# Reordering one step of an edge-gated graph layer: the add a tile ahead, expansion first, aggregation last

## The chip, the cores and the metric

The kernel runs on one core of a Trainium2 chip. The metric is the device time of one execution in microseconds (us); lower is better. Five engines work side by side: TensorE (PE in the profile, with its weight loads as PEld), VectorE (DVE), ScalarE (ACT), GpSimd (POOL, here the issuer of gathers) and SyncE (SP, an issuer of plain transfers). Each works through its own list of instructions in order and waits for others by semaphores.

## The reference

For each of 16 batches, 1024 nodes with 256 features `h`. Every pair of nodes (u, v) gets a gate, and the adjacency `A`, which is nearly empty (about nine entries per node, the diagonal among them), weighs it:

```python
pre_u = h @ W1[:256];  pre_v = h @ W1[256:]
hidden = relu(pre_u[:, :, None] + pre_v[:, None, :] + b1)
S = sigmoid(hidden @ W2 + b2)                 # one number for each u, v
a_t = einsum('buv,bud->bvd', S * A, h)        # gated sum over u
m_t = einsum('uv,bud->bvd', A, h) * h         # plain sum over u
out = beta1*h + beta2*(a_t @ Wa + ba) + beta3*(m_t @ Wm + bm)
```

## The kernel before

Only pairs with a non-zero adjacency are computed. The edges of a node tile of 128 v are put into lists, 10 tiles of up to 128 edges: two windows (`w`) of 64 v, five tiles (`j`) each. Batches go in four groups of four. One group with one node tile is a **block** (32 in all), one edge tile of a block is a **step** `n` (10 to a block, 320 in all); `s` is n mod 10. For a whole group the kernel first writes a table with a row of 2,048 numbers for each node u: `pre_u` of the four batches and, behind it, `h` of the four batches. Tables of later groups and lists of later node tiles are made in between the steps of earlier ones, up to about step 233.

Per step there are these pieces, all functions inside the kernel:

- `fetch(n)` (L496, POOL): an indirect DMA gathers the 128 table rows of the edges into one of six buffers `fetched`. It can start when the step that used the buffer six tiles ago is aggregated.
- `expand(n)` (L569, PE): two products with a 0/1 matrix `mark` spread `pre_v + b1`, which lies in `X`, over the edges, into one of two PSUM tiles `pc`.
- `gate(n)` (L601, L606 on DVE; L609, L612 on ACT): VectorE adds the gathered `pre_u` and `pc` into a tile `t`; four products, one per batch, take the ReLU times `W2` and sum along the row into `sc`. ScalarE takes the sigmoid `gt` and scales, once per batch, the weights in the tile `left`.
- `left_adj(n)` (L579, ACT): the unscaled half of `left`, the adjacency values at their places.
- `aggregate(n)` (L623, PE): products of `left` with the gathered `h`, 8 instructions where the tile touches one quarter of the window (j = 0 and 4), 16 where it touches two; they accumulate in PSUM in `acc0` and `acc1`.
- `half_end` (L631, ACT): after j = 2 and j = 4, thus after n with s = 2, 4, 7 and 9, a finished half is copied out of PSUM into `ev`.

Beside these a step holds work for whole blocks. What TensorE makes there is copied by ScalarE: transposes of `ev` into `LT` (L641, L644) at s = 1 (for the block before), 7 (two halves) and 9; the output products (L672, copies to `z` L675) at s = 3 to 6; the next block's `X` and its split `low` (L427, L461, L462 at s = 0 and 2, casts L465 at 3 and L468 at 5 and 6); table rows (L427, L443), in the middle of the run at s = 1 and 8; at s = 1 and 6 ScalarE also makes the next `mark` (L562). VectorE's part of it (L654, L676, L463) and the output transfers are put off by one to three steps through `after` and come up in `do(n)`.

The order of instructions on each engine is written by hand (`manual_schedule`): it is the order in which the main loop calls these functions. In step n the loop calls aggregate(n-1), two gathers of adjacency values (`fetch_val`, L382), fetch(n+5), half_end where due, gate(n), left_adj(n+1), load_mark, do(n), expand(n+2), and then the block's work.

Of the kernel before, what the change touches and what calls it, by code (L numbers as in the profile page):

```python
# [7 lines left out]
FP = mybir.dt.float32  # L8
# [3 lines left out]
ALU = mybir.AluOpType  # L12
AX = mybir.AxisListType
P = 128
# [3 lines left out]
def kernel(  # L18
# [42 lines left out]
    nc = tc.nc  # L61
    B, N, D = x.shape
    NT = N // P
    DC = D // P
    GB = 4
    NG = B // GB
    GD = GB * D
    W = 64
    NW = P // W
    TW = 5  # L70
# [58 lines left out]
    MID = TW // 2  # L129
# [81 lines left out]
    one = main.enter_context(tc.tile_pool(name="one", bufs=1))  # L211
# [17 lines left out]
    NF = 6  # L229
    EARLY = 4  # L230
    fetched = []
# [147 lines left out]
    def fetch_val(n):  # L379

        for i, j in wanted[:n]:
            nc.gpsimd.indirect_dma_start(  # L382
                out=val[:, i, j:j + 1], out_offset=None, in_=adj_flat,
                in_offset=bass.IndirectOffsetOnAxis(ap=vidx[:, i, j:j + 1], axis=0),
                bounds_check=N * N - 1, oob_is_err=False)
        del wanted[:n]
# [91 lines left out]
    def go(gen, step):  # L478

        try:  # L480
            gen.send(step)
        except StopIteration:
            pass
# [5 lines left out]
    def where(n):  # L489
        k, s = divmod(n, T)  # L490
        w, j = divmod(s, TW)
        return k, *order[k], w, j

    def fetch(n):
        k, g, vt, w, j = where(n)
        nc.gpsimd.indirect_dma_start(  # L496
            out=fetched[n % NF], out_offset=None, in_=table[g],
            in_offset=bass.IndirectOffsetOnAxis(ap=uidx[:, vt * NW + w, j:j + 1], axis=0),
            bounds_check=N - 1, oob_is_err=False)
# [55 lines left out]

    marks, pcs, accs, evs, hbs, LTs, lefts = {}, {}, {}, {}, {}, {}, {}

    def load_mark(q):  # L560
        marks[q] = big.tile([P, E], FR, name="mark")
        nc.scalar.copy(marks[q], whose[:, order[q // NW][1] * NW + q % NW, :])  # L562

    def expand(n):
        k, g, vt, w, j = where(n)
        pcs[n] = psc.tile([P, GD], FP, name="pc")
        for h in range(2):
            c = slice(2 * h * D, (2 * h + 2) * D)
            nc.tensor.matmul(pcs[n][:, c], marks[n // TW][:, j * P:(j + 1) * P], cuts[k][:, w, c],  # L569
                             start=True, stop=True)  # L570


    def left_adj(n):
        k, g, vt, w, j = where(n)
        i = vt * NW + w
        m = len(QUARTERS[j])
        o = max(2 * j - 1, 0)
        lefts[n] = wk.tile([P, 2, GB, 2, V], FP, name="left")
        nc.scalar.activation(lefts[n][:, :m, :, 0, :], onehot[:, i, o:o + m, :].unsqueeze(2).to_broadcast([P, m, GB, V]),  # L579
                             AF.Copy, scale=val[:, i, j:j + 1])  # L580
# [11 lines left out]
    def fill(n, gap=True):  # L592
        for r in running:
            if r[1] == gap and r[2] <= n:
                piece_of(r, n)
                break

    def gate(n):
        k, g, vt, w, j = where(n)
        t = one.tile([P, GB, D], FP, name="t")  # L600
        nc.vector.tensor_tensor(t, fetched[n % NF][:, :GD].rearrange("p (b d) -> p b d", b=GB),  # L601
                                pcs.pop(n).rearrange("p (b d) -> p b d", b=GB), ALU.add)
        sc = wk.tile([P, GB], FP, name="sc")
        for b in range(GB):
            fill(n)
            nc.vector.scalar_tensor_tensor(t[:, b, :], t[:, b, :], 0.0, w2_b,  # L606
                                           ALU.max, ALU.mult, accum_out=sc[:, b:b + 1])
        gt = wk.tile([P, GB], FP, name="gt")
        nc.scalar.activation(gt, sc, AF.Sigmoid, bias=b2_b)  # L609
        for b in range(GB):  # L610
            m = len(QUARTERS[j])
            nc.scalar.activation(lefts[n][:, :m, b, 1, :], lefts[n][:, :m, b, 0, :], AF.Copy, scale=gt[:, b:b + 1])  # L612

    def aggregate(n):
        k, g, vt, w, j = where(n)
        left, f = lefts.pop(n), fetched[n % NF]
        for i, q in enumerate(QUARTERS[j]):
            h, r = divmod(q, 2)
            first = j == h * MID and r == 0
            if first:  # L620
                accs[h] = psa.tile([P, 2, D], FP, name=f"acc{h}")
            for b in range(GB):
                nc.tensor.matmul(accs[h][b * 2 * V:(b + 1) * 2 * V, r, :],  # L623
                                 left[:, i, b].rearrange("p k v -> p (k v)"), f[:, GD + b * D:GD + (b + 1) * D],
                                 start=first, stop=(j == q + 1), skip_group_check=True)


    def half_end(n, q):

        evs[q] = one.tile([P, 2, D], FP, name=f"ev{q}")  # L630
        nc.scalar.copy(evs[q], accs.pop(q))  # L631
# [110 lines left out]
        expand(n)  # L742
    left_adj(0)
    total = BS * T
    for n in range(total + 2):
        k, s = divmod(n, T)
        if 1 <= n <= total:
            aggregate(n - 1)
            fetch_val(2)
            if n - 1 + NF < total:  # L750
                fetch(n - 1 + NF)
            if n % TW in (0, MID + 1):
                half_end(n - 1, 0 if n % TW else 1)
        if n < total:
            gate(n)
            if n + 1 < total:
                left_adj(n + 1)
        if n % TW == 1 and n // TW + 1 < total // TW:
            load_mark(n // TW + 1)
        do(n)  # L760
        if n + 2 < total:
            expand(n + 2)
        if n == 1:
            w_a = load_weights(Wa, "w_a", nc.sync)
            w_m = load_weights(Wm, "w_m", nc.sync)
            bias = load_rows(bm, D, "bias", nc.sync)
            ba_b = load_rows(ba, D, "ba_b", nc.sync)
            be1 = load_rows(beta1, 1, "be1", nc.sync)
            be2 = load_rows(beta2, 1, "be2", nc.sync)
            be3 = load_rows(beta3, 1, "be3", nc.sync)  # L770
            after(10, scale_late)
        if s == 0 and 0 < k < BS:
            hbs[k - 1] = big.tile([P, GB, D], FP, name="h_blk", bufs=1)
            g, vt = order[k - 1]
            nc.sync.dma_start(hbs[k - 1], x_rows[vt * P:(vt + 1) * P, g * GB:(g + 1) * GB, :])
        if n == total - 6:
            hbs[BS - 1] = hts.tile([P, GB, DC, P], FP, name="hT").rearrange("p b c n -> p b (c n)")
            for v, m, f in tails:
                for h, o in tail_rows(x, v, m, f):
                    nc.sync.dma_start(h, o)  # L780
        for i in advance.get(n, ()):
            next(made[i], None)
        if n in start_list:
            running.append([made[start_list[n]], True, n])
            piece_of(running[-1], n)
        fill(n, False)
        if (s == 1 and 0 < k < BS) or n == total:
            turn_over(k - 1, 1, 1, n)
        if s in (3, 4, 5, 6) and 0 < k < BS:
            if s == 3:  # L790
                end = block_end(k - 1)
                next(end)
            go(end, n)
        if s == 7 and k < BS:
            turn_over(k, 0, 0, n)
            turn_over(k, 0, 1, n)
        if s == 9 and k < BS:
            turn_over(k, 1, 0, n)
        if n == total - 2:
            end = tail(tails[:2], n)  # L800
            next(end)
        elif n == total - 1:
            go(end, n)
        elif n >= total:
            end = tail([tails[2 + n - total]], n)
            next(end)
            go(end, n)
            go(end, n)
        if k + 1 < BS and s in (0, 2, 3, 5, 6):
            if s == 0:  # L810
                parts = halves(k + 1)
                next(parts)
            go(parts, n)
        if n in loads:
            if loads[n] in begun and loads[n][0] == 1:
                aside_.remove(loads[n])
            load_hT(loads[n])
            if loads[n] not in begun:
                copy_h(loads[n])
                begun.add(loads[n])  # L820
        if n in at:
            if at[n] != last:
                last = at[n]
                piece = rows(last)
                next(piece)
            go(piece, n)
        if n == 120:
            nc.gpsimd.partition_all_reduce(longest, rest, P, bass_isa.ReduceOp.max)
            after(n + 12, count_rest)
# [7 lines left out]
    with tc.If(any_left > 0):  # L837
        with ExitStack() as s2:
# [3 lines left out]
            for vt in range(NT):  # L842
# [21 lines left out]
                with tc.For_i(0, n_turns, 1):  # L864
# [9 lines left out]
                    for g in range(NG):  # L874
# [4 lines left out]
                        sc = fw.tile([P, GB], FP, name="fb_sc")  # L879
# [64 lines left out]
```

## Time and profile before

| | |
|---|---|
| time, median of 3 runs | 1151.51 us (1146.13 to 1153.36) |
| profiled execution, span from first to last instruction | 1165.8 us (its own device time is not given apart) |
| PE busy | 1092.1 us, 94% |
| DVE busy | 1056.2 us, 91% |
| ACT busy | 893.5 us, 77% |
| POOL busy | 439.9 us, 38% |
| data moved | 391.40 MB, mean 336 GB/s |
| mean granted TensorE clock | 0.976 |

A line of a group names the line of the kernel, the engine and operation, what is written and read, and how often; then its busy time in us, the mean of one in ns, and the idle time just before such instructions with what ended it. A line of the waits has the waiting instruction, the one that released it, the time in total, how often and the longest. A line of the timeline has start and length in us, then the instructions, merged where the same follow each other (`x4`); a bracket gives the idle time ahead of them.

### The profile page before, as it was taken

The numbers are of one execution on the slowest core, as the hardware profiler recorded it, in microseconds if no ns is written. First come the engines' busy times: TensorE is split into PE (matmuls) and PEld (weight loads), VectorE is DVE, ScalarE is ACT, GpSimd is POOL, SyncE is SP. The second block draws the span as 40 slices with busy tenths as digits, with TensorE's granted clock in tenths as the row PEclk, the third lists the DMA queues.
The fourth block names the chain that finished last, engine by engine and source line by source line (L and its number), as shares of the span: only waits on it lengthen the run. The fifth ranks groups of instructions, "written<-read, shape, count | busy, mean of one in ns | idle before, by whom it ended". The sixth has DMA issues, their size and how long they took to land. (4 is left out here: it accounts for less than half of the span.)

```text
span 1165.8 us, 23918 instructions
## 1 busy us (share of the span) xinstructions
PE 1092.1 (94%) x7633; PEld 723.1 (62%) x7633; DVE 1056.2 (91%) x3487; ACT 893.5 (77%) x2624; POOL 439.9 (38%) x428
## 2 busy tenths in 40 slices
PE   7867899999999999999999999999999999999986
PEld 6744666666666666666666666666666666666553
DVE  7688889888999989999999999999999999999994
ACT  2346587767887878888888888888888888888873
POOL 1556645253335333443333333333333333333330
PEclk9868899999999999999999999999999999999999
DMA  9986898999999999999999999999998998999991
GB/s 286 298 307 223 277 372 312 362 320 331 342 320 323 396 379 336 358 350 402 389 374 369 355 364 356 360 364 383 371 375 324 361 322 333 334 339 328 328 346 60
DMA packets 147048, 391.40 MB, mean 336 GB/s; under 512 B 16753, under 2 KB 105329, under 8 KB 110705
## 3 DMA queue, kind: packets, MB, share of 16 engines
q0 software_dynamic: 50016, 300.50, 68.9%
q1 hardware_dynamic: 81616, 74.99, 20.0%
q10 hardware_dynamic: 15280, 14.29, 3.7%
q8 instruction: 63, 1.03, 0.3%
q14 instruction: 73, 0.59, 0.1%
HBM read 393.78 MB, written 50.33 MB: 381 GB/s over the span
## 5 line engine op out<-in xcount | busy, mean ns | idle before, releaser
L496 POOL DMA_INDIRECT fetched<-table,uidx x320 | 341.5, 1067 | 628.3 <-PE acc L623 447.2
L606 DVE SCALAR_TENSOR_TENSOR t<-t,w_b 128x256 f32<-128x256 f32 x1280 | 478.3, 421 | 19.3 <-ACT left L612 0.5
L601 DVE TENSOR_TENSOR t<-fetched,pc 128x1024 f32<-128x1024 f32 x320 | 389.3, 1217 | 41.4 <-PE pc L569 13.9
L623 PE MATMUL acc<-fetched,left 128*32 128x256 f32 x4096 | 336.2, 391 | 31.9 <-ACT left L612 26.2
L612 ACT ACTIVATE left<-left,gt 128x32 f32<-128x32 f32 (+1 forms) x1280 | 299.3, 304 | 10.4
L569 PE MATMUL pc<-X,mark 128*128 128x512 f32 x640 | 237.6, 453 | 6.2 <-ACT mark L562 5.0
L623 PEld LDWEIGHTS acc<-fetched,left 128*32 128x32 f32 x4096 | 130.6, 109 | 179.3 <-issue 52.4
L569 PEld LDWEIGHTS pc<-X,mark 128*128 128x128 f32 x640 | 97.2, 191 | 140.0 <-issue 89.3
L609 ACT ACTIVATE gt<-sc,b_b 128x4 f32<-128x4 f32 x320 | 96.2, 301 | 43.4 <-DVE t L606 40.8
L672 PE MATMUL misc<-w_m,LT 128*128 128x256 f32 x496 | 117.2, 379 | 0.0
L672 PE MATMUL misc<-w_a,LT 128*128 128x256 f32 x496 | 117.1, 379 | 0.0
L579 ACT ACTIVATE left<-onehot,val 128x128 f32<-128x128 bf16 (+1 forms) x320 | 116.5, 364 | 0.0
L427 PE MATMUL misc<-w_v,hT 128*128 128x256 f32 x448 | 107.3, 383 | 0.0
L427 PE MATMUL misc<-w_u,hT 128*128 128x256 f32 x416 | 101.2, 390 | 5.7 <-ACT few L329 3.6
L606 DVE DVE_READ_ACCUMULATOR t<-t,w_b 128x1 f32 x1280 | 104.0, 81 | 0.0
L672 PEld LDWEIGHTS misc<-w_a,LT 128*128 128x128 f32 x496 | 93.9, 189 | 15.1
L672 PEld LDWEIGHTS misc<-w_m,LT 128*128 128x128 f32 x496 | 93.8, 189 | 14.9
L382 POOL DMA_INDIRECT val<-in_adjT_dram,vidx x80 | 85.7, 1071 | 35.1 <-issue 22.4
L427 PEld LDWEIGHTS misc<-w_v,hT 128*128 128x128 f32 x448 | 86.0, 192 | 13.9
L427 PEld LDWEIGHTS misc<-w_u,hT 128*128 128x128 f32 x416 | 79.5, 195 | 17.3 <-ACT few L329 3.7
L631 ACT COPY ev<-acc 128x512 f32<-128x512 f32 x128 | 75.5, 590 | 14.6 <-PE acc L623 4.2
L675 ACT COPY z<-misc 128x512 f32<-128x512 f32 x62 | 36.3, 586 | 58.1 <-PE misc L672 38.8
(164 smaller groups left out, 947.9 us busy)
## 6 DMA issues: line engine op xcount, KB each, us to landing
h_blk<-in_x_dram SPq DMA_DIRECT2D x31, 512.0 KB
out_dram<-z SPq DMA_DIRECT2D x31, 512.0 KB
hT<-in_xT_dram SPq DMA_DIRECT2D x28, 512.0 KB
table<-in_x_dram ACTq DMA_DIRECT2D x24, 512.0 KB
table<-tab SPq DMA_DIRECT2D x24, 512.0 KB
fetched<-table,uidx POOLq DMA_INDIRECT x320
table<-in_x_dram SPq DMA_DIRECT2D x8, 512.0 KB
table<-fetched SPq DMA_DIRECT2D x8, 512.0 KB
```

The source lines that it names most:

```text
L382: nc.gpsimd.indirect_dma_start(out=val[:, i, j:j + 1], out_offset=None, in_=adj_flat, in_offset=bass.IndirectOffsetOnAxis(ap=vidx[:, i, j: ...
L427: nc.tensor.matmul(p[:, bb * D:(bb + 1) * D], hT[:, 2 * h + bb, i, :], wt[:, i, :], start=(i == 0 and not begun), stop=(i == DC - 1), skip ...
L496: nc.gpsimd.indirect_dma_start(out=fetched[n % NF], out_offset=None, in_=table[g], in_offset=bass.IndirectOffsetOnAxis(ap=uidx[:, vt * NW ...
L569: nc.tensor.matmul(pcs[n][:, c], marks[n // TW][:, j * P:(j + 1) * P], cuts[k][:, w, c], start=True, stop=True)
L579: nc.scalar.activation(lefts[n][:, :m, :, 0, :], onehot[:, i, o:o + m, :].unsqueeze(2).to_broadcast([P, m, GB, V]), AF.Copy, scale=val[:, ...
L601: nc.vector.tensor_tensor(t, fetched[n % NF][:, :GD].rearrange("p (b d) -> p b d", b=GB), pcs.pop(n).rearrange("p (b d) -> p b d", b=GB), ...
L606: nc.vector.scalar_tensor_tensor(t[:, b, :], t[:, b, :], 0.0, w2_b, ALU.max, ALU.mult, accum_out=sc[:, b:b + 1])
L609: nc.scalar.activation(gt, sc, AF.Sigmoid, bias=b2_b)
L612: nc.scalar.activation(lefts[n][:, :m, b, 1, :], lefts[n][:, :m, b, 0, :], AF.Copy, scale=gt[:, b:b + 1])
L623: nc.tensor.matmul(accs[h][b * 2 * V:(b + 1) * 2 * V, r, :], left[:, i, b].rearrange("p k v -> p (k v)"), f[:, GD + b * D:GD + (b + 1) * D ...
L631: nc.scalar.copy(evs[q], accs.pop(q))
L672: nc.tensor.matmul(pz[:, bb * D:(bb + 1) * D], LTs[k][:, c, 2 * h + bb, i, :], wt[:, c, :], start=False, stop=(i == 0 and c == DC - 1), sk ...
```

## The change

VectorE's add becomes a function of its own, `add(n)`, that writes in place of the gathered half of the buffer; the tile `t` is gone, and the four products work in the buffer too. `add(0)` runs ahead of the loop, and step n then calls add(n+1) before the products of n. The scalings move to a function `weigh(n)`. The aggregation with its fetches and `half_end` moves to `gather_in`. Step n now calls expand(n+2), add(n+1), gate(n), load_mark, do(n), the block's work, gather_in(n-1), weigh(n), left_adj(n+1).

```diff
+    def add(n):
+        t = fetched[n % NF][:, :GD]
+        nc.vector.tensor_tensor(t, t, pcs.pop(n), ALU.add)
+
     def gate(n):
         k, g, vt, w, j = where(n)
-        t = one.tile([P, GB, D], FP, name="t")
-        nc.vector.tensor_tensor(t, fetched[n % NF][:, :GD].rearrange("p (b d) -> p b d", b=GB),
-                                pcs.pop(n).rearrange("p (b d) -> p b d", b=GB), ALU.add)
+        t = fetched[n % NF][:, :GD].rearrange("p (b d) -> p b d", b=GB)
         sc = wk.tile([P, GB], FP, name="sc")
         for b in range(GB):
             fill(n)
             nc.vector.scalar_tensor_tensor(t[:, b, :], t[:, b, :], 0.0, w2_b,
                                            ALU.max, ALU.mult, accum_out=sc[:, b:b + 1])
+        scs[n] = sc
+
+    def weigh(n):
+        k, g, vt, w, j = where(n)
+        sc = scs.pop(n)
         gt = wk.tile([P, GB], FP, name="gt")
         nc.scalar.activation(gt, sc, AF.Sigmoid, bias=b2_b)
...
     total = BS * T
+    add(0)
+
+    def gather_in(n):
+        aggregate(n)
+        fetch_val(2)
+        if n + NF < total:
+            fetch(n + NF)
+        if (n + 1) % TW in (0, MID + 1):
+            half_end(n, 0 if (n + 1) % TW else 1)
+
     for n in range(total + 2):
         k, s = divmod(n, T)
-        if 1 <= n <= total:
-            aggregate(n - 1)
-            fetch_val(2)
-            if n - 1 + NF < total:
-                fetch(n - 1 + NF)
-            if n % TW in (0, MID + 1):
-                half_end(n - 1, 0 if n % TW else 1)
+        if n == total:
+            gather_in(n - 1)
+        if n + 2 < total:
+            expand(n + 2)
         if n < total:
+            if n + 1 < total:
+                add(n + 1)
             gate(n)
-            if n + 1 < total:
-                left_adj(n + 1)
         if n % TW == 1 and n // TW + 1 < total // TW:
             load_mark(n // TW + 1)
         do(n)
-        if n + 2 < total:
-            expand(n + 2)
...
+        if n < total:
+            if n:
+                gather_in(n - 1)
+            weigh(n)
+            if n + 1 < total:
+                left_adj(n + 1)
```

More of the change, by code (lines that the diff above doesn't have):

```diff
@@ L553, in scale_late @@
         nc.vector.tensor_scalar(w_m, w_m, be3, None, ALU.mult)
+    scs = {}
     marks, pcs, accs, evs, hbs, LTs, lefts = {}, {}, {}, {}, {}, {}, {}
```

## The prediction

> **What bounds the kernel now.** I read the page's engine shares first, then the groups, the waits of a middle stretch, and the timeline of TensorE (PE) and ScalarE (ACT).
>
> ```profile
> PE 1092.1 (94%) x7633; PEld 723.1 (62%) x7633; DVE 1056.2 (91%) x3487; ACT 893.5 (77%) x2624; POOL 439.9 (38%) x428
> ...
> L606 DVE SCALAR_TENSOR_TENSOR t<-t,w_b 128x256 f32<-128x256 f32 x1280 | 478.3, 421 | 19.3 <-ACT left L612 0.5
> L601 DVE TENSOR_TENSOR t<-fetched,pc 128x1024 f32<-128x1024 f32 x320 | 389.3, 1217 | 41.4 <-PE pc L569 13.9
> ```
>
> TensorE and VectorE (DVE) are both near full, so small bubbles decide. VectorE's waits from 310 to 870 us:
>
> ```profile
> DVE t L601 <- PE pc L569: 3.3, 9, 0.5
> DVE key L249 <- DMA key<-in_adjT_dram: 2.8, 1, 2.8
> DVE t L601 <- DMA fetched<-table,uidx: 2.1, 2, 1.7
> ```
>
> In 560 us it waits some 10 us for others. Now TensorE from step 6 to step 8 of a block (a block is ten steps; n is the tile, s = n mod 10):
>
> ```profile
> 601.72 1.89 PE L672 MATMUL misc<-w_m,LT 128*128 128x256 f32 x8
> 603.54 1.07 PE L623 MATMUL acc<-fetched,left 128*32 128x256 f32 x16
> 604.54 0.73 PE L569 MATMUL pc<-X,mark 128*128 128x512 f32 x2
> 605.11 1.03 PE L641 MATMUL misc<-ident,ev 128*128 128x128 f32 x8
> 606.08 1.65 PE L623 MATMUL acc<-fetched,left 128*32 128x256 f32 x16
> 607.65 0.73 PE L569 MATMUL pc<-X,mark 128*128 128x512 f32 x2
> 608.95 1.69 PE L623 MATMUL acc<-fetched,left 128*32 128x256 f32 x16 [0.56 <-ACT left L612]
> ```
>
> and ScalarE beside it:
>
> ```profile
> 602.75 0.71 ACT L562 CAST mark<-whose 128x640 fp32r<-128x640 uint8 x1
> 603.65 0.59 ACT L675 COPY z<-misc 128x512 f32<-128x512 f32 x1 [0.19 <-PE misc L672]
> 604.26 1.05 ACT L468 CAST X<-low 64x1024 fp32r<-64x1024 f32 x1
> 605.33 0.30 ACT L609 ACTIVATE gt<-sc,b_b 128x4 f32<-128x4 f32 x1
> 605.66 0.96 ACT L612 ACTIVATE left<-left,gt 128x32 f32<-128x32 f32 x4
> ...
> 606.82 1.04 ACT L644 COPY LT<-misc 128x512 f32<-128x512 f32 x2
> 607.76 0.59 ACT L631 COPY ev<-acc 128x512 f32<-128x512 f32 x1
> 608.24 0.30 ACT L609 ACTIVATE gt<-sc,b_b 128x4 f32<-128x4 f32 x1
> 608.57 0.96 ACT L612 ACTIVATE left<-left,gt 128x32 f32<-128x32 f32 x4
> ```
>
> An aggregation of 16 products takes 1.07 us when its scalings are there, 1.65 when it must follow them as they come: the stall sits inside "busy". It ends where a step's products are few and ScalarE's chain (copies, sigmoid, four scalings) is longer than what TensorE has left to do.
>
> Summing TensorE's start-to-start distances at their undisturbed values over all steps gives 31.1 us of work per block in n = 60 to 239 (18 blocks), which takes 32.7; from n = 240 (8 blocks), where no table rows are made, 27.7 of 31.2. The rest is stall. VectorE's floor per block, from the timeline's distances: add to first product 10 x 1.26, between products 30 x 0.35, last product to what follows 4.3, and the block's own work (z 2 x 0.66, low 1.14, LT 2 x 0.60) 3.7, together 31.0. So **VectorE sets the last 8 blocks, and the TensorE-ScalarE loop, closely followed by VectorE, the 18 in the middle**.
>
> **What the Trainium skill says.** "Perfetto Trace Analysis", Per-engine timelines: a matmul's end in a profile is estimated, not observed; agreed, the 1.65 above is spread starts. "TensorE: Matmul & The Clock Gate", Architectural detail: ScalarE and VectorE are strict first-in first-out; agreed: VectorE finished tile 147's products at 601.87, but its sigmoid starts at 605.33, behind mark, z and cast. "VectorE: DVE Perf Modes", The DRAIN you can't avoid: a semaphore after each VectorE operation costs nothing. This trace differs: an add followed by its own products, which wait for it, is 1.24 to 1.33 us from start to start, and 1.14 when an unrelated operation follows; a product followed by the next add is 0.52, by an unrelated operation 0.35. "DMA: Bandwidth & Descriptors", Specifications: 16 engines reach 435 GB/s; the page has 336 on average, 402 in its best slice.
>
> **The change, part by part.** VectorE's adds, products, scalings and matmuls keep their number and size.
>
> *The add one tile ahead, in place.* The stream becomes add(n+1), products(n). Neither waits for the instruction just before it, so about 0.12 per add and 0.17 on half of the last products go: 0.2 us a step, VectorE's floor falls from 31.0 to 29.0 per block. In the last 8 blocks this is worth up to 2 us each, if nothing else is late; in the middle nothing, as the loop of TensorE and ScalarE binds at once. Dropping tile t costs nothing: the add wrote 1,024 elements before too.
>
> *TensorE's order.* Before, cyclically: aggregate(n-1), expand(n+2), products(n). After: aggregate(n-1), expand(n+3), products(n+1). Only the pairing shifts: **each aggregation now follows the next step's products, and ScalarE's ev copy, sigmoid and scalings of n come behind the copies of step n, no longer of n-1**. I walked one block both ways with the timeline's distances (products 0.215 each, aggregation 0.26 or 0.69 from first to last start, expansion 0.335 + 0.23, hand-over to or from an aggregation 0.31; on ScalarE 0.48 per 128x512 copy, cast 1.07, mark 0.62, sigmoid 0.33, scalings 0.96, left 0.29; matmul to copy 0.42; the last start of a delayed 16-product aggregation 0.73 after the last scaling). The walk of before gives 32.1 in the middle (one stall of 0.6, at aggregate(7)) and 30.8 at the end, against 32.7 and 31.2 measured. The walk of after:
> - s = 1: L641's transposes need ev of the aggregation that was issued just one expansion earlier, and ev waits behind X and low. From the last product of s = 0: copies at 0.42 and 0.90, ev 1.38 to 1.97, transposes 2.02; TensorE is free at 1.44. Stall 0.58. Before, a whole step lay between. Behind it stand rows, aggregate(0) and all the rest of TensorE's queue.
> - aggregate(6): ScalarE does ev(4), sigmoid and scalings(5), left, mark, z, cast, sigmoid and scalings(6) without a break; TensorE has only aggregate(5) (8 products), an expansion and 8 transposes (1 us) after z's products. Stall 1.2.
> - s = 9: transposes behind ev of aggregate(7): 0.19. aggregate(8): the chain ev, sigmoid, scalings takes 2.9 from aggregate(7)'s start, TensorE has an expansion and four transposes: 0.66.
>
> Sum 2.6 stalled instead of 0.6, on 31.4 of work in either walk: 34.05 a block. Against the 32.7 measured that is 1.35; against the walk of before 2.0, if its 0.6 of unexplained stalls stays. I take 1.7: 18 x 1.7 = 30.6 us. At the end, where s = 1 and 8 have no rows, aggregate(0) and (7) stall as well (0.6 and 0.8): 31.9 against 31.2, 8 x 0.7 = 5.6 us; the shorter VectorE floor is spent on this. For the first 6 blocks, full of list-making, I did no walk: the s = 1 and aggregate(6) stalls add 1.8, VectorE's relief may take 2 back. Bounds -6 to +12 us, taken 6.
>
> *Fetches.* L496 and L382 on POOL follow the aggregation, now a step later, while the add comes earlier. From issue to add was 10.6 to 13.7 us (group means of 60 steps); it becomes two steps and an expansion, 7.5. Landing isn't in the views; counting the gather queue's 8 KB packets, rows land some 7.5 us after issue (medians of stretches 6.8 to 7.8), rarely later than 9. Adds will wait up to 2.5 us, products(n) behind them on VectorE. That costs nothing while sigmoid(n) starts 4 us later than its scores, as the walk has it; without that cover up to 1 us a step. At the start, the seventh fetch comes a step later: 2 us. SP's transfers keep their order; left has three buffers and its reader is done a step earlier.
>
> Sum: 30.6 + 5.6 + 6 + 2 = 44 us on the profiled span of 1165.8, 3.8%. The page gives that execution's span alone, and it is 1.2% over the median 1151.5. So 1151.5 x 1.038 = **1195 us**.
>
> **The rivals.**
> *VectorE's relief comes through (faster).* Mechanism: the saved 0.2 us a step, with stalls on TensorE no longer than today's. For it: VectorE waits for almost nothing, and several aggregations gain longer products in front. Price: the middle falls to the walk's 32.1 (18 x 0.6 = 11), the end to 30.8 (3), the beginning 6: 20 us, 1131. It decides once the new order stalls less than 1.3 us in a middle block; below that each 0.1 gives 2 us. Against it: s = 1 and aggregate(6) alone make 1.8.
> *A wash.* ScalarE's waits for products (22.5 us for X, 20.1 for z between 310 and 870) shrink as its chain stalls, and half of my 2.6 is hidden: 31.4 + 1.3 is the 32.7 of now, 1152.
> *Gathers bind (slower still).* If adds wait beyond the 4 us of cover, 320 x 0.12 = 38 more: 1233. For it: from 150 to 900 us the windows show DMA 0.94 to 1.01 busy. Against: a slower pace asks less of it.
>
> **How the numbers follow.** Forecast 0.64, own range 1172 to 1222 (walk differences of 1.0 and 2.6 a block); faster rival 0.17; wash 0.12; gathers 0.07. About 1% is what a measurement of this kernel can tell from no change. Faster 0.17, same 0.12, slower 0.71. The range must leave out no more than 0.2: from 1136, which takes in the wash and the weak end of the faster case, to 1225.
>
> **What would show it.** L641's first transposes at s = 1 and 9 waiting for ACT ev, which they hardly did (0.8 us in all); aggregate(6) stretched or waiting for left, aggregate(7) in the middle blocks no longer; add to product distance 1.14; ScalarE's waits for DVE t at L609 near zero; more DVE waits for fetched. If blocks in the middle take under 32.5 us, the walk is wrong, most likely in ScalarE's chain between ev(4) and scalings(6).

## The result, and the profile after

The changed kernel takes 1199.72 us (median of four runs, 1197.41 to 1202.25) where the kernel before, run beside it, takes 1150.30 us (1146.13 to 1153.36). The ratio is 1.0438, with a 95% interval of 1.0409 to 1.0466: **4.4% slower**. The prediction was 1195 us, slower by 3.8%. Its profiled execution took 1197.41 us with a span of 1195.6 us.

First the page of the changed kernel: engine shares, then groups that answer to those shown of before.

```profile
PE 1104.9 (92%) x7633; PEld 725.2 (61%) x7633; DVE 1024.8 (86%) x3487; ACT 887.2 (74%) x2624; POOL 438.5 (37%) x428
...
L601 DVE TENSOR_TENSOR fetched<-fetched,pc 128x1024 f32<-128x1024 f32 x320 | 388.5, 1214 | 131.5 <-DMA fetched<-table,uidx 84.2
L609 DVE SCALAR_TENSOR_TENSOR fetched<-fetched,w_b 128x256 f32<-128x256 f32 x1280 | 475.4, 418 | 0.0
...
L639 ACT COPY ev<-acc 128x512 f32<-128x512 f32 x128 | 75.6, 591 | 66.6 <-PE acc L631 64.3
...
L617 ACT ACTIVATE gt<-sc,b_b 128x4 f32<-128x4 f32 x320 | 96.3, 301 | 20.8 <-DVE fetched L609 19.0
...
L649 PE MATMUL misc<-ident,ev 128*128 128x128 f32 x512 | 74.1, 277 | 18.9 <-ACT ev L639 15.0
```

VectorE is 31 us less busy than in the profile of before (1024.8 against 1056.2), and that buys nothing: it now waits 84.2 us for gathered rows (`fetched`). The transposes of L649 wait 15.0 us for ScalarE's copies `ev` (0.8 before), and these wait 64.3 us for the aggregations.

VectorE's waits in the middle, from 310 to 870 us, of the changed kernel:

```profile
DVE fetched L601 <- DMA fetched<-table,uidx: 44.0, 36, 3.9
DVE fetched L601 <- PE misc L427: 8.5, 3, 3.6
DVE fetched L601 <- PE acc L631: 7.6, 5, 3.7
DVE fetched L601 <- PE pc L570: 1.9, 6, 0.5
```

Before it waited some 10 us there, now 62. Next TensorE in the changed kernel: first the transposes at s = 9 of block 14 and at s = 1 of block 15, then block 15 from s = 6 to 9:

```profile
618.34 0.73 PE L570 MATMUL pc<-X,mark 128*128 128x512 f32 x2
618.91 0.60 PE L649 MATMUL misc<-ident,ev 128*128 128x128 f32 x4
...
625.36 0.73 PE L570 MATMUL pc<-X,mark 128*128 128x512 f32 x2
626.51 0.66 PE L649 MATMUL misc<-ident,ev 128*128 128x128 f32 x4 [0.42 <-ACT ev L639]
...
645.60 0.64 PE L631 MATMUL acc<-fetched,left 128*32 128x256 f32 x8
646.17 0.73 PE L570 MATMUL pc<-X,mark 128*128 128x512 f32 x2
646.74 1.03 PE L649 MATMUL misc<-ident,ev 128*128 128x128 f32 x8
648.34 1.69 PE L631 MATMUL acc<-fetched,left 128*32 128x256 f32 x16 [0.56 <-ACT left L620]
...
652.34 1.07 PE L631 MATMUL acc<-fetched,left 128*32 128x256 f32 x16
653.34 0.74 PE L570 MATMUL pc<-X,mark 128*128 128x512 f32 x2
653.92 0.60 PE L649 MATMUL misc<-ident,ev 128*128 128x128 f32 x4
654.45 1.55 PE L631 MATMUL acc<-fetched,left 128*32 128x256 f32 x16
```

and ScalarE beside it, in block 15:

```profile
624.89 0.59 ACT L461 CAST X<-misc 128x512 fp32r<-128x512 f32 x1 [1.67 <-PE misc L427]
625.38 0.59 ACT L462 COPY low<-misc 128x512 f32<-128x512 f32 x1
625.85 0.60 ACT L639 COPY ev<-acc 128x512 f32<-128x512 f32 x1
...
643.44 0.58 ACT L639 COPY ev<-acc 128x512 f32<-128x512 f32 x1 [1.28 <-PE acc L631]
643.92 0.30 ACT L617 ACTIVATE gt<-sc,b_b 128x4 f32<-128x4 f32 x1
644.25 0.90 ACT L620 ACTIVATE left<-left,gt 128x16 f32<-128x16 f32 x4
645.06 0.38 ACT L580 ACTIVATE left<-onehot,val 128x128 f32<-128x128 bf16 x1
645.35 0.71 ACT L563 CAST mark<-whose 128x640 fp32r<-128x640 uint8 x1
645.97 0.57 ACT L683 COPY z<-misc 128x512 f32<-128x512 f32 x1
646.56 1.05 ACT L468 CAST X<-low 64x1024 fp32r<-64x1024 f32 x1
647.64 0.30 ACT L617 ACTIVATE gt<-sc,b_b 128x4 f32<-128x4 f32 x1
647.97 0.96 ACT L620 ACTIVATE left<-left,gt 128x32 f32<-128x32 f32 x4
```

The three new stalls can be read off. *Transposes at s = 1*: expansion to transposes is 0.57 us undisturbed (at s = 9, 618.34 to 618.91) and 1.15 here (625.36 to 626.51), because `ev` runs until 626.4 behind X and low. *aggregate(6)*: ScalarE works without a break from 643.44 through eight pieces of work before the scalings at 647.97; TensorE has only 8 products, an expansion and 8 transposes meanwhile, waits, and then follows the scalings one by one (1.69 instead of 1.07). *aggregate(8)*: stretched to 1.55. In return aggregate(7), which took 1.65 us in the lines of before (606.08), takes 1.07 (652.34).

For all blocks I took TensorE's start-to-start distances less their undisturbed values, as the prediction did; this gives work and stall per block. The kernel before is shown in two profiles: the one that the prediction used, and one from a chip like the one on which the result was measured (run r12 below).

| us per block | before, first profile | before, r12 | after |
|---|---|---|---|
| blocks 0 and 1 | 43.67 | 38.48 | 40.27 |
| blocks 2 to 5 | 37.78 | 38.46 | 39.81 |
| blocks 6 to 23 | 32.77 | 32.57 | 33.85 |
| of it stall | 1.70 | 1.50 | 2.79 |
| of these, blocks 15 to 23 | 31.91 | 31.96 | 33.47 |
| blocks 24 to 30 | 31.10 | 31.11 | 31.48 |
| from expand(312) to the end, in all | 47.0 | 47.1 | 51.8 |

In blocks 6 to 23 the stall of after is made of aggregate(6) 1.29 (0.0 in the first profile of before), the transposes 0.66 (0.13), aggregate(8) 0.41 (0.28) and aggregate(7) 0.17 (0.85). Lists are still made in blocks 6 to 14; the row on blocks 15 to 23 shows the order by itself.

### The profile page after: what moved, and what is told of

Same layout as the page of the kernel before. It is cut to its first block, busy times and chain, and to the rows that moved or that the text cites. A ratio compares the mean times of both kernels' runs of the same rounds, so it can differ in the third digit from the quotient of the medians.

```text
span 1195.6 us, 24015 instructions
## 1 busy us (share of the span) xinstructions
PE 1104.9 (92%) x7633; PEld 725.2 (61%) x7633; DVE 1024.8 (86%) x3487; ACT 887.2 (74%) x2624; POOL 438.5 (37%) x428
## 4 chain that ended last, share of the span: by engine, by line
PE 61%; ACT 17%; DVE 10%; DMA 7%; issue 3%; POOL 0%; ACTq 0%; POOLq 0%; DVEq 0%
PE acc L631 18%; PE misc L427 15%; PE misc L680 12%; PE pc L570 10%; DMA fetched<-table,uidx 5%; ACT left L620 4%; DVE fetched L609 3%; DVE fetched L601 3%; PE misc L649 2%; ACT ev L639 2%; ACT X L468 2%; PE misc L431 2%; ACT gt L617 1%; ACT mark L563 1%; ACT X L461 1%
## 5 line engine op out<-in xcount | busy, mean ns | idle before, releaser
L496 POOL DMA_INDIRECT fetched<-table,uidx x320 | 340.6, 1064 | 659.7 <-PE acc L631 484.1
L601 DVE TENSOR_TENSOR fetched<-fetched,pc 128x1024 f32<-128x1024 f32 x320 | 388.5, 1214 | 131.5 <-DMA fetched<-table,uidx 84.2
L609 DVE SCALAR_TENSOR_TENSOR fetched<-fetched,w_b 128x256 f32<-128x256 f32 x1280 | 475.4, 418 | 0.0
L631 PE MATMUL acc<-fetched,left 128*32 128x256 f32 x4096 | 339.7, 390 | 26.9 <-ACT left L620 25.8
L631 PEld LDWEIGHTS acc<-fetched,left 128*32 128x32 f32 x4096 | 133.5, 109 | 175.8 <-issue 66.0
L639 ACT COPY ev<-acc 128x512 f32<-128x512 f32 x128 | 75.6, 591 | 66.6 <-PE acc L631 64.3
L680 PEld LDWEIGHTS misc<-w_m,LT 128*128 128x128 f32 x496 | 94.6, 191 | 16.7 <-DVE LT L662 1.7
L609 DVE DVE_READ_ACCUMULATOR fetched<-fetched,w_b 128x1 f32 x1280 | 101.6, 79 | 0.0
L461 ACT CAST X<-misc 128x512 fp32r<-128x512 f32 x64 | 37.5, 586 | 82.9 <-PE misc L427 82.9
L382 POOL DMA_INDIRECT val<-in_adjT_dram,vidx x80 | 85.3, 1066 | 33.7 <-issue 19.2
L649 PE MATMUL misc<-ident,ev 128*128 128x128 f32 x512 | 74.1, 277 | 18.9 <-ACT ev L639 15.0
```

Of the source, the lines that this page charges most:

```text
L496: nc.gpsimd.indirect_dma_start(out=fetched[n % NF], out_offset=None, in_=table[g], in_offset=bass.IndirectOffsetOnAxis(ap=uidx[:, vt * NW ...
L601: nc.vector.tensor_tensor(t, t, pcs.pop(n), ALU.add)
L631: nc.tensor.matmul(accs[h][b * 2 * V:(b + 1) * 2 * V, r, :], left[:, i, b].rearrange("p k v -> p (k v)"), f[:, GD + b * D:GD + (b + 1) * D ...
L649: nc.tensor.transpose(pt[:, i * P:(i + 1) * P], ev[:, r, c * P:(c + 1) * P], ident)
L680: nc.tensor.matmul(pz[:, bb * D:(bb + 1) * D], LTs[k][:, c, 2 * h + bb, i, :], wt[:, c, :], start=False, stop=(i == 0 and c == DC - 1), sk ...
```

## The experiments

Chips differ, so every run is read as a ratio to the kernel before on its own chip: there it took 1166.34 us for r1 to r4, 1147.89 for r5 to r8, 1170.53 for r9 to r11 and 1150.57 for r12.

My theory after the result: the order on TensorE and ScalarE costs the time, by the three stalls, and the add ahead is a small gain or nothing. Rivals: VectorE's add is what costs; gathers that now come late are what costs.

### The parts of the change, one by one

**r2_add_alone**: the kernel before, with the add one tile ahead and in place; the order of TensorE and ScalarE stays.

```diff
+    def add(n):
+        t = fetched[n % NF][:, :GD]
+        nc.vector.tensor_tensor(t, t, pcs.pop(n), ALU.add)
...
+    add(0)
     for n in range(total + 2):
...
+            if n + 1 < total:
+                add(n + 1)
             gate(n)
```

> The kernel before with VectorE's part alone: add one tile ahead, in place; TensorE's and ScalarE's order as before. Theory (the loss comes from the order on TensorE and ScalarE): the middle blocks fall to the walk's 32.1 and the last ones to 30.8, so 5 to 20 us faster than before, 1130 to 1145. Rival A (the add ahead is what costs, by waiting for gathers with the products behind it): slower than before, 1165 to 1200.

Measured: 1186.69 us, ratio 1.0161 (1.0121 to 1.0202). **My theory missed: the add ahead alone makes the kernel slower.** The time is that of rival A, but its cause isn't: the adds wait 19.3 us for gathered rows, and four times as long for the expansions. Two groups of its page:

```profile
L600 DVE TENSOR_TENSOR fetched<-fetched,pc 128x1024 f32<-128x1024 f32 x320 | 389.4, 1217 | 120.3 <-PE pc L569 77.1
...
L611 ACT ACTIVATE gt<-sc,b_b 128x4 f32<-128x4 f32 x320 | 95.9, 300 | 106.6 <-DVE fetched L608 94.6
```

VectorE's adds wait 77.1 us for the expansions (13.9 in the first profile of before), and ScalarE's sigmoids wait 94.6 us for VectorE; in the first profile of before it was 40.8:

```profile
ACT gt L609 <- DVE t L606: 40.8, 52, 2.5
```

One such place in VectorE's timeline of r2_add_alone:

```profile
599.08 0.42 DVE L608 SCALAR_TENSOR_TENSOR fetched<-fetched,w_b 128x256 f32<-128x256 f32 x1
599.42 0.08 DVE L608 DVE_READ_ACCUMULATOR fetched<-fetched,w_b 128x1 f32 x1
600.73 1.22 DVE L600 TENSOR_TENSOR fetched<-fetched,pc 128x1024 f32<-128x1024 f32 x1 [1.23 <-PE pc L569]
601.87 0.42 DVE L608 SCALAR_TENSOR_TENSOR fetched<-fetched,w_b 128x256 f32<-128x256 f32 x1
```

The add of tile n+1 waits 1.23 us for TensorE; the products of tile n, which have all that they need, stand behind it; the sigmoid and the scalings of n wait for them in turn. The saving itself came as worked out: add to first product is 1137 ns (median; 1256 in r12). Blocks 15 to 23 go from 31.97 us (r1, on the same chip) to 32.60.

**r10_in_place**: the kernel before, with the add in place but in its old position.

```diff
-        t = one.tile([P, GB, D], FP, name="t")
-        nc.vector.tensor_tensor(t, fetched[n % NF][:, :GD].rearrange("p (b d) -> p b d", b=GB),
-                                pcs.pop(n).rearrange("p (b d) -> p b d", b=GB), ALU.add)
+        t = fetched[n % NF][:, :GD].rearrange("p (b d) -> p b d", b=GB)
+        nc.vector.tensor_tensor(fetched[n % NF][:, :GD], fetched[n % NF][:, :GD], pcs.pop(n), ALU.add)
```

> The kernel before with one edit: the add writes in place of the gathered half of its buffer, and stays where it was, directly ahead of its own products. Theory: what made the add alone (one tile ahead, in place) 1.6% slower than before is its being ahead: the add of tile n+1 waits for the products of expand(n+1) with the block products of tile n queued behind it. So in place alone is between 0.6% faster and 0.7% slower than before (ratio 0.994 to 1.007). Rival (writing in place is what costs, because the add then holds the gathered buffer in another way): 1 to 1.6% slower, ratio 1.010 to 1.016.

Measured: 1163.27 us, ratio 0.9947 (0.9930 to 0.9964). So writing in place is a gain of 0.5%, and what costs in r2_add_alone is that the add is *ahead*. Where the gain sits: last product to next add is 346 ns (median; 519 in r12), because the add no longer writes the tile that the product before it still reads; blocks 24 to 30, which VectorE sets, take 30.48 us instead of 31.1.

**r3_order_alone**: the change, but VectorE adds in the old way, into `t` and in the step of its products.

```diff
-    add(0)
...
+        if n < total:
+            add(n)
...
-            if n + 1 < total:
-                add(n + 1)
             gate(n)
```

(and `add` writes a tile `t` as before)

> The changed order on TensorE and ScalarE alone; VectorE adds tile n into t right ahead of its own products, as before. Theory: the three new stalls are all there, 1192 to 1210, like the change. Rival A: near before, 1145 to 1160.

Measured: 1205.43 us, ratio 1.0336 (1.0290 to 1.0382), as expected. Blocks 6 to 23 take 34.07 us, with aggregate(6) stalling 1.27, the transposes 0.63, aggregate(8) 0.42: the same stalls as in the change. The order alone makes most of the loss. (It moves TensorE's and ScalarE's work and the issue of the gathers together; no run takes these apart.)

**r11_order_in_place**: the change, with the add in place but in its own step, not ahead (`add(0)` and `add(n + 1)` go, `add(n)` stands at the top of step n).

> The change with one edit: the add stays in place of the gathered half, but is made in its own step, directly ahead of its own products, not a step ahead. Theory: the reordering of TensorE and ScalarE makes nearly all of the loss (3.4% without the add's change, 4.3% with it), and the add ahead about 1% on top, through later gathers: ratio to before 1.030 to 1.037. Rival 1 (the add ahead costs nothing inside the change): 1.041 to 1.046, as the change itself. Rival 2 (the add ahead is a gain inside the change, as the shorter distances on VectorE would have it): above 1.047.

Measured: 1201.60 us, ratio 1.0284 (1.0238 to 1.0329), just below the 1.030 to 1.037 expected of the theory and far from both rivals. The parts now add up: the order 1.0336 times in place 0.9947 is 1.0281, measured 1.0284; and the add *ahead* makes the rest, 1.0284 to the 1.0430 of the change (r5), 1.4% (by the two intervals, 0.9 to 1.9%). These ratios come from three chips, each to the kernel before on its own.

Where chips hardly differ, the parts can be compared in the profiles themselves. In blocks 15 to 23 the four profiles of before take 31.88 to 31.97 us a block, and r3, r11 and the change 33.47, 33.49 and 33.47: there the order makes all of the loss, and neither the add in place nor the add ahead changes anything. In blocks 24 to 30, r11 and the change take 31.49 and 31.48. So what the add ahead costs in the new order lies elsewhere: blocks 2 to 5 take 38.12 us in r11 (before 37.78 to 38.46) and 39.81 in the change, the stretch after expand(312) 49.3 and 51.8, some 9 us in all; the rest of the 1.4% can't be placed, as r11 ran on a chip of the slower kind (see r12).

The adds of r11_order_in_place and its sigmoids:

```profile
L601 DVE TENSOR_TENSOR fetched<-fetched,pc 128x1024 f32<-128x1024 f32 x320 | 389.1, 1216 | 74.4 <-DMA fetched<-table,uidx 47.3
...
L617 ACT ACTIVATE gt<-sc,b_b 128x4 f32<-128x4 f32 x320 | 96.4, 301 | 2.5 <-DVE fetched L609 1.0
```

Its adds wait 47.3 us for gathers, those of the change 84.2; its sigmoids wait 1.0 us for VectorE, those of the change 19.0. In the new order, too, the add comes ahead of its inputs, but of the two it is mostly the gathered rows that come last. (The expansions are not far ahead of them: r6 below.)

### The suspects by themselves

**r5_after_again**: the change once more, beside the next runs.

> The change once more, beside the kernels below on one chip, since the kernel before differs by 15 us between chips. Theory: 3 to 4.5% slower than before on the same chip; blocks 6 to 23 at 33.7 to 34.1 us, their stalls at L649, aggregate(6) and aggregate(8) as in the first profile (0.66, 1.29, 0.41).

Measured: 1196.88 us, ratio 1.0430 (1.0405 to 1.0454). Blocks 6 to 23 take 33.86 us, 24 to 30 take 31.50: the table of after again.

**r6_half_gather**: the change, but each gather brings rows of 4 KB, into the half of the buffer that `h` goes to. The half for `pre_u` is left out, so the adds work on what lies in the buffer and depend on no gather at all; and as the row numbers stay, the rows that come aren't the `h` of the edges.

```diff
-            out=fetched[n % NF], out_offset=None, in_=table[g],
+            out=fetched[n % NF][:, GD:], out_offset=None, in_=table[g].rearrange("n (t d) -> (n t) d", t=2),
```

> The change with each gathered row half as long (4 KB in place of 8 KB, into the half that the aggregation reads; the sums of the first half are left out, the add works on what lies there). It takes 150 of 391 MB off the transfers. Theory (order): VectorE's waits for gathers fall from 84 us to under 15, the stalls on TensorE stay: within 1.5% of the change. Rival B (gathers bind): 2.5% or more faster than the change, the three stalls shrink.

Measured: 1180.22 us, ratio 1.0270 (1.0249 to 1.0291), 1.4% faster than the change beside it (r5). VectorE's waits from 310 to 870 us are now a single line:

```profile
DVE fetched L601 <- PE pc L570: 57.5, 95, 1.4
```

No add waits for a gather. Now they wait for the expansions, 57.5 us in 95 short waits, which the rows had hidden; TensorE's blocks in the middle hardly notice. Against r5 the spans differ by 14.8 us: 7.3 in blocks 2 to 5 (37.78 instead of 39.60 each), 4.5 after expand(312) (46.5 instead of 51.0), 2.7 in blocks 6 to 23 (33.71 instead of 33.86), and nothing in blocks 24 to 30 (31.49). In blocks 6 to 23 the three stalls stay: aggregate(6) 1.25, transposes 0.66, aggregate(8) 0.41. So late gathers cost the change at most some 17 us, mainly near the start and at the end, and the stalls on TensorE are no consequence of them. "At most", because halving the bytes relieves every other transfer too, and because not all that is won is waiting: from r5 to r6 TensorE's mean granted clock goes from 0.97 to 0.98 in blocks 2 to 5, and from 0.91 to 0.96 after expand(312). In the profile of the change, one group of eight products behind a wait takes 3.55 us, where the same eight take 1.89 elsewhere (in r6, for one, at 1143.74); the mean granted clock from 1157 to 1162 us is 0.66:

```profile
1157.91 3.55 PE L680 MATMUL misc<-w_m,LT 128*128 128x256 f32 x8 [1.25 <-DVE LT L662]
```

Whether late rows bring this lower clock about is not shown.

**r4_no_ev_wait**: the change, but the transposes of L649 read a constant matrix in place of `ev`, so that they wait for no copy; what the lists have summed doesn't enter the output.

```diff
-            nc.tensor.transpose(pt[:, i * P:(i + 1) * P], ev[:, r, c * P:(c + 1) * P], ident)
+            nc.tensor.transpose(pt[:, i * P:(i + 1) * P], upto[:, i * P:(i + 1) * P], ident)
```

> The change, with the transposes reading a constant tile in place of ev, so the gated and plain sums are left out of the result; the copies to ev stay. It takes away the wait of L649 for ev alone. Theory: 0.66 us a block in the middle and end, 2 in blocks 2 to 5, is 25 us at most, part of which comes back as a longer stall of aggregate(0) and (8) right behind: 1176 to 1190. Rival A or gathers as the bound: 1195 to 1202, no change.

Measured: 1202.54 us, ratio 1.0315 (1.0274 to 1.0356), against 1.043 of the change. The expected time was written for the chip of the result; as a ratio, the gain is about 1.1%, 13 us, near the low end of what was expected. The transposes' stall falls from 0.66 to 0.05 us a block, and blocks 15 to 23, which no list-making disturbs, go from 33.47 to 32.92, 5 us of the 13; the rest can't be placed, as the two runs met different chips. In blocks 24 to 30 nothing is won (31.49): the 0.65 us that is taken away there comes back at aggregate(0), whose stall grows from 0.52 to 1.17. **In this kernel a stall that is removed is worth its time only if the next aggregation's scalings are already there.**

**r7_mark_moved**: the change, but `load_mark` comes at s = 0 and 5 instead of 1 and 6, which takes one cast of about 0.6 us out of ScalarE's chain ahead of aggregate(6).

```diff
-        if n % TW == 1 and n // TW + 1 < total // TW:
+        if n % TW == 0 and n // TW + 1 < total // TW:
```

> The change with the load of the next mark one step earlier (s = 0 and 5 in place of 1 and 6), where ScalarE waits for X, or for an aggregation. It takes 0.62 us out of ScalarE's unbroken chain in front of aggregate(6) and nothing else. Theory: the stall of aggregate(6) falls from 1.27 to some 0.7, 0.6 x 25 blocks = 12 to 17 us faster than the change, 1 to 1.4%. Rival B: no change within 0.4%.

Measured: 1189.40 us, ratio 1.0347 (1.0314 to 1.0380), 0.6% faster than r5 by the medians, or 7.5 us (0.8% by the ratios). The direction is right and the size about half: aggregate(6) stalls 1.06 us instead of 1.28, where about 0.7 was expected. That the chain carries this stall is shown. What takes up the rest of the cast stands in the trace of r7, block 15:

```profile
647.00 0.39 ACT L580 ACTIVATE left<-onehot,val 128x128 f32<-128x128 bf16 x1
647.65 0.59 ACT L683 COPY z<-misc 128x512 f32<-128x512 f32 x1 [0.26 <-PE misc L680]
648.26 1.04 ACT L468 CAST X<-low 64x1024 fp32r<-64x1024 f32 x1
```

Without the cast of mark, the copy to `z` comes so early that it waits for TensorE's products: from `left` to `z` it is 0.65 us instead of 0.91 (645.06 to 645.97 in the change), so 0.26 of the 0.62 are won.

### A better kernel, and the kernel before on other chips

**r8_better**: the kernel before, in its old order, with edits in the direction that the experiments gave: mark at s = 0 and 5, the cast of s = 6 ahead of the copy to z, `ev` behind the scalings, and the add in place but not ahead.

```diff
...
+        t = fetched[n % NF][:, :GD].rearrange("p (b d) -> p b d", b=GB)
+        nc.vector.tensor_tensor(fetched[n % NF][:, :GD], fetched[n % NF][:, :GD], pcs.pop(n), ALU.add)
...
-            if n % TW in (0, MID + 1):
-                half_end(n - 1, 0 if n % TW else 1)
...
-        if n % TW == 1 and n // TW + 1 < total // TW:
+        if 1 <= n <= total and n % TW in (0, MID + 1):
+            half_end(n - 1, 0 if n % TW else 1)
+        if n % TW == 0 and n // TW + 1 < total // TW:
...
+        if k + 1 < BS and s == 6:
+            go(parts, n)
...
-        if k + 1 < BS and s in (0, 2, 3, 5, 6):
+        if k + 1 < BS and s in (0, 2, 3, 5):
```

> The kernel before with three moves on ScalarE and one on VectorE: mark loaded at s = 0 and 5; at s = 6 the cast L468 ahead of the copy to z; the copies to ev behind the scalings of the same step; the add in place (not ahead). By the theory that the TensorE-ScalarE loop sets the middle: aggregate(7) there stalls under 0.3 in place of 0.85, aggregate(8) of the last blocks 0.4 less, 10 to 20 us faster than before (1 to 1.7%). If gathers or VectorE set the middle: within 0.7% of before.

Measured: 1139.75 us, ratio 0.9920 (0.9902 to 0.9937): **0.8% faster than the kernel before**, some 8 us where 10 to 20 were expected. Blocks 6 to 23 take 32.41 us (aggregate(7) stalls 0.18 instead of 0.71 in r12), 24 to 30 take 30.64. r10 shows that the add in place alone gives 0.5%; the rest of r8's edits together are worth some 0.3%, by the intervals of two chips anything from nothing to 0.5%.

**r1_before_again** and **r9_before_profile**: the kernel before without an edit, to see why its first profile, of 1165.8 us, lies 1.3% over the median of before on the chip of the result.

> The kernel before, unchanged, for a second profile. The first profiled execution had a span 15 us over the median of the timed runs. If that is an accident of its start, this span is near 1150 and blocks 6 to 23 still take 32.4 to 32.8 us each with their stall at aggregate(7); the first two blocks (87 us in the first profile) are shorter by some 10 us. If middle blocks are what differs, they come out at 32.1, the walk's value.

> The kernel before once more, for a profile on the same chip as the two runs beside it. Theory: blocks 6 to 23 and 24 to 30 take the same time per block as in the first profile of before (32.8 and 31.1 us, within 0.3), since those stretches are set by the order of the work; what differs between executions is in the first six blocks. Rival (all of the span differs in proportion): the middle blocks differ by as many per cent as the span does.

Measured: r1 1172.41 us with a span of 1170.5; r9 1168.56 with 1166.7. Blocks 6 to 23 take 32.81 and 32.75 us, 24 to 30 take 31.04 and 31.06, as in the first profile; blocks 0 and 1 take 45.08 and 43.80 (43.67 in the first profile). So r1's first idea, an accident of the start of one execution, fell: these chips are slow at the start each time.

**r12_before_third**: the kernel before again, on whichever chip it met.

> The kernel before unchanged, for one more profile; on which chip it lands is left to chance. The profiles so far fall into two classes: on chips where before takes 1166 to 1171 us the first two blocks take 43.7 to 46.0 us each, whatever the version, and on the chip where before takes 1148 us those of the change and its variants take 38.7 to 41.6. Theory: chips differ in the first six blocks (list-making) and not in the order-bound rest. So on a chip with before near 1150, blocks 0 and 1 take 36 to 41 us each and blocks 6 to 23 still 32.75 within 0.15; on a chip with before near 1168 all is as in the earlier profiles (43.7 to 45.1, and 32.75). Rival (a chip is slower throughout): on a chip with before near 1150 the middle blocks take 32.3 us or less.

It met a chip where before takes 1150.57 us, and took 1156.93 with a span of 1155.0. Blocks 0 and 1 take 38.48 us each, 5 less than on the slower chips; blocks 6 to 23 take 32.57 (0.03 below the bound I had set, far above the rival's 32.3), 24 to 30 take 31.11. The 0.2 us between 32.57 and the 32.77 of the first profile lies in blocks 7 and 11: 32.4 us in r12, 34.7 to 35.2 in the other three profiles. In blocks 2 to 5 r12 is the slower one (38.46 against 37.78 to 38.16), and in blocks 15 to 23 the four profiles agree within 0.1. So the chips, each met with one batch of runs, differ where lists are made, and not in the order-bound rest. The mean granted clock doesn't explain it: in blocks 0 and 1 it was 0.90 in r5, which took 41.6 us a block, and 0.91 in r11, which took 44.6. Why they differ stays open. A trace of it: between 73 and 150 us the profiles of the slower chips have waits for a releaser that the trace can't name, 14.7 us at L644 in r1, 3.8 at L461 and 4.7 at L496 in r9, and r12 has none.

With r12 the change can be read like with like. Its profile of 1155.0 becomes 1195.6 after: 3.6 us in blocks 0 and 1, 5.4 in 2 to 5, 23.0 in 6 to 23, 2.6 in 24 to 30, 4.7 after expand(312), and 1.2 before the first block: 40.5 of the 40.6. The medians differ by more, 49.4 us: r12's profiled execution was 6 us longer than the run timed beside it, and that of the change the fastest of its four. So 9 us of the result lie in no profile.

## Why the prediction was right, point by point

**The bound and the walk: right.** The order of TensorE and ScalarE sets the middle. The walk gave 2.6 us of stall a block, measured 2.79; the transposes 0.77 at s = 1 and 9, measured 0.66 (0.58 at s = 1 in the lines above, the very number of the walk); aggregate(6) 1.2, measured 1.29; aggregate(8) 0.66, measured 0.41. A block after was to take 34.05, measured 33.85. That aggregate(7) would no longer be stretched in the middle holds (0.85 to 0.17), and at the end it is (0.76). Runs show the cause for two of the three stalls, r7 for aggregate(6) and r4 for the transposes; that of aggregate(8) is read from the timeline alone.

**The middle's difference: too large.** 1.7 a block was a choice between 1.35 and 2.0; measured 1.28 against r12 and 1.08 against the first profile, so 23.0 or 19.4 us where 30.6 stood. In blocks 15 to 23 it is 1.5 (33.47 less 31.96), near the 1.7. In blocks 6 to 14 it is 1.06 (34.23 less 33.17 in r12): in two of them, 6 and 9, after is even the shorter one (33.7 against 34.7, 34.6 against 35.4), since before loses 1.2 to 1.5 us at aggregate(7) there, against 0.57 in most blocks, and after nothing. The walk had no such blocks in it.

**The last 8 blocks: 5.6 us predicted, 7.3 measured, but put together otherwise.** In blocks 24 to 30 only 0.37 a block was lost, not 0.7; 4.7 us lie after expand(312), and r6, with half the gathers, gets 4.5 us back there. VectorE's shorter stream was spent on stalls, as forecast.

**The start: the bounds hold.** 6 us for the first six blocks, 9.0 measured; 2 for the seventh fetch, 1.2 measured before the first block.

**The add ahead: the step that failed, outside the middle.** The prediction put its waits at "That costs nothing while sigmoid(n) starts 4 us later than its scores". The distances fell as said (1133 ns from add to product, 1.14 predicted), and adds wait for gathers as said. Where the cover was walked, it holds: in blocks 6 to 23 adds wait 50.9 us for rows, 40 times, r6 wins back only 2.7 us there, and blocks 15 to 23 take the same time with and without the add ahead (r11). But a walk of a middle block was taken for all blocks: in blocks 2 to 5 six waits sum to 13.7 us, up to 4.2 instead of the 2.5 worked out, and r6 wins back 7.3; after expand(312) it wins back 4.5. In all, put ahead, the add costs 1.4% in the new order, and 2.1% in the old one (1.0161 over 0.9947). In the sum the term for fetches should have been up to 15 us instead of 0, half of which lies in the first blocks, and in place should have been a gain of 0.5%.

**So the total is near partly by luck.** The order alone was worked out at 42 us (30.6 + 5.6 + 6), 3.6%, and is 3.4%; that part is right for the reason given. The add's part was put at nothing and is 0.9% (in place -0.5%, ahead +1.4%). Together 4.3 to 4.4% instead of 3.8%, inside the range: a middle priced too high and an add priced too low cancel in part.

**The rivals.** VectorE's relief needed less than 1.3 us of stall in a middle block; there are 2.79. The wash counted on ScalarE's waits for X and z to shrink: those for z do (20.1 to 8.5 us between 310 and 870), those for X double (22.5 to 45.2). Gathers that bind were priced at 38 us and cost at most 17.

**Scaling by the ratio: right.** The first profile of before was of 1165.8 us, and its blocks 0 and 1 are those of the slower chips (43.67 us); the ratio to it, 3.8%, could be carried over, its absolute time not.

## What to carry to other kernels

Walk the pairing, not the busy time: when an order is shifted, write down for each consumer what its producer's engine still has in front of it, with distances from the timeline; here that gave 2.6 us of stall a block where 2.79 came. An instruction that is put ahead on an in-order engine needs *both* its inputs a step earlier, and what stands behind it pays for the later one, unless the wait is covered, as in the middle here; saving 0.12 us an instruction did not buy that. And look for the part of a change that needs no reordering: the add in place, without the rest, is the piece that gains.

## What the runs showed of the hardware that I had not expected

- One program differs by 1.4 to 2% between chips (1148 to 1151 us and 1166 to 1171 us, one batch of runs on each), and the difference sits where lists are made: 38.5 against 43.7 to 45.1 us in each of the first two blocks, 32.4 against 34.7 to 35.2 in blocks 7 and 11, and 31.0 to 31.1 in blocks 24 to 30 on both.
- A VectorE instruction that overwrites what the one before it still reads starts 0.17 us later than one that doesn't (519 and 346 ns from start to start). The add in place avoids it, and this is worth 0.5% of the kernel.
- Removing 0.65 us of TensorE's wait in each of the last blocks (r4) moved their time by nothing (31.48 to 31.49).
